# Feed-forward keys and receptance in two scaled float16 parts, and a fourth buffer for the attention probabilities

## The chip, the cores and the metric

The kernel runs on one core of one Trainium2 chip. The metric is device microseconds of one execution. The kernel before was run three times: 1599.81, 1601.11 and 1602.56 us, median 1601.11. One more execution was profiled: its own time is 1597.72 us, its span from the first to the last instruction 1595.9 us. The core has a matrix engine (TensorE, PE in the profile, with its weight loads shown as PEld), and VectorE (DVE), ScalarE (ACT), GpSimd (POOL) and a queue that issues transfers (SP).

## The reference

The input x has 4 rows of 2048 tokens with 256 channels. Four residual layers follow one another, each on a layer norm of x:

```python
x = x + attn_a(layernorm(x))      # (W n + b) of token 1 of each row, added to all its tokens
x = x + ffn(layernorm(x))         # weights W_r, W_k, W_v, mu_r, mu_k
x = x + attn_b(layernorm(x))      # 16 heads of 64, rotary positions, window of 128 back
x = x + ffn(layernorm(x))         # the same weights again
```

The feed-forward layer mixes each token n with the token before it:

```python
xr = mu_r * n + (1 - mu_r) * n_prev;   xk = mu_k * n + (1 - mu_k) * n_prev
out = sigmoid(xr @ W_r.T) * (relu(xk @ W_k.T) ** 2 @ W_v.T)
```

The attention attends in blocks of 128 tokens to the block itself and the one before, under a band mask, with a softmax.

## The kernel before, in words

The 8192 tokens are worked on in 32 groups of 256 (two tiles of 128). Each group passes through named stages, each of several steps: x (load, and the first layer's addition), f0 (first feed-forward), ln (layer norm for attention), v0 to v3 (values), q0 to q3 (queries and keys of four heads each, with rotary tables), s0 to s3 (attention of four heads each), o (output projection), f1 (second feed-forward), sv (store). The last group is split into two halves at its end (f1, f2 and w0, w1).

A matrix product in nearly float32 precision is made from parts: an operand a is cast to a hi part, and its lo part is a minus hi; three products hi x hi, hi x lo and lo x hi are summed in PSUM. In attention the parts are float16 and the weights are scaled by powers of two ahead of time. In the feed-forward layers of the kernel before all parts are float32r, four bytes each.

The steps of a feed-forward (class Ffn, lines 943 to 1123) are, with their engines: st sums of the norm (DVE), rs its scale (POOL), xn normalised tokens (ACT), tr transposes (PE), xt copy to SBUF and hs the column of the token before (ACT), d difference to the token before, xm and xo the mixes for receptance and key (DVE), xh hi part of both (ACT, 128x1024), xl lo part (POOL), pk keys (PE, 12 matmuls), pr receptance (PE, 12), rl relu, sq square, kh hi part of the keys (ACT), kl lo part (DVE), th tanh of half the receptance (ACT; the sigmoid is (1 + tanh)/2), pv values (PE, 12), sg the gate (DVE), ad addition to x (POOL).

The steps of an attention quarter (class Att, line 1332) are ks mask and sc scores into four PSUM banks (PE); for each head h of four m the maximum (DVE), e the exponential (ACT, two instructions in place in PSUM), h hi part (ACT) and l lo part (DVE) of the probabilities, into a tile phl for two heads; t0 and t1 the transposing transfers from phl to a tile pt (SP); av the product with the values (PE); i and n the division (DVE), ch and cl the parts of the context (ACT, POOL), tc its transposing transfer. In the queries and keys (class Qk, line 1223) qm and km are matmuls (PE), ka and kb the two products with the rotary tables (DVE), ad their sum (POOL), hi and lo the parts (ACT, POOL). For q1 the second product is made by ke (a copy on ACT) and mu (POOL). ks and kp hand keys on to the next group.

PSUM is divided into six single banks (tag pp) and one pair of banks (tag pair) which the query and key products and the context products take in turn. BUFS (line 38) gives the number of buffers of each tag; phl and pt have three each.

The order of the work is written out ahead by a planner (class Plan, line 143). Each step has a line in its class's SPEC with engine, duration in us, what it needs, which buffers it takes and which it gives back. The planner steps through a list schedule; among steps that could begin at about the same time on an engine the one with the lowest rank goes first. A rank is the group's number times PERIOD plus an entry of the table RANK (line 51), with another entry for each stage of the first and the last five groups. The instructions are then emitted in that order, each engine's queue keeps it, and waits are on the tiles that the instructions share. Since every instruction passes through one recording helper, nearly all have line 276 in the profile; tiles tell them apart: f_xm, f_xh, f_xl, f_pk, f_pr, f_kk, f_sg, f_pv belong to Ffn, at_s, at_mn, at_phl, at_pt, at_cx, at_c, at_ct to Att, qk_pd, qk_A, qk_B, qk_q, qk_k to Qk, pv to the values, po to the output. In the middle of the run several groups are in work at once: around group g's output stand s3 of group g+1, q0 of g+3 and f0 of g+4.

The class Setup (line 457) prepares the weights: the feed-forward steps there are fr, fk, fv (loads), mu (1 - mu), frh, fkh, fvh (hi parts, ACT), frl, fkl, fvl (lo parts, POOL), and fvs (W_v times 0.5, for the sigmoid).

Of the kernel before, what the change touches and what calls it, by code (L numbers as in the profile page):

```python
# [18 lines left out]
P = 128  # L19
C = 256  # L20
# [9 lines left out]
WSC = 256.0  # L30
EXPO = 0x7F800000
# [8 lines left out]
        "cs": 2, "A": 2, "B": 2, "q": 3, "k": 3, "mn": 3, "phl": 3, "pt": 3,  # L40
# [11 lines left out]
    "p.c1": -5056.91, "p.c2": 2969.02, "p.c3": -4885.05, "p.lv": -3111.05, "p.lb": -2925.83, "p.lw": -5009.81,  # L52
    "p.lo": -413.49, "p.lk": -2678.25, "p.lm": 2640.67, "p.lq": -3077.55, "p.fk": -1972.19, "p.fr": -2838.78,
    "p.fv": -777.00, "p.bd": -2779.47, "p.nvs": 3014.63, "p.nvm": 3072.90, "p.nvr": -2978.83, "p.nks": -788.22,
    "p.nkm": -4306.80, "p.nkr": -83.63, "p.nqs": -5037.35, "p.nqm": -4939.68, "p.nqr": -774.36, "p.sc": -472.11,
    "p.wv0": 570.16, "p.xv0": -201.89, "p.yv0": 3153.22, "p.zv0": -4686.76, "p.wv1": -2600.05, "p.xv1": -3342.91,
    "p.yv1": -610.29, "p.zv1": -4852.83, "p.wk0": -3021.86, "p.xk0": -1892.46, "p.yk0": -821.64, "p.zk0": -2369.83,
    "p.wk1": -2733.80, "p.xk1": -83.69, "p.yk1": -1953.56, "p.zk1": -2430.55, "p.wq0": -168.05, "p.xq0": 2297.47,
    "p.yq0": -4898.14, "p.zq0": -5081.41, "p.wq1": 2689.14, "p.xq1": -2913.52, "p.yq1": 3363.58, "p.zq1": -5071.63,
    "p.mk": -3071.43, "p.mu": -2906.24, "p.frh": -2530.67, "p.frl": -2423.55, "p.fkh": -2983.12, "p.fkl": 3185.31,  # L60
    "p.fvs": -769.81, "p.fvh": -4579.58, "p.fvl": 3091.15, "p.oq": -3006.79, "p.om": -204.90, "p.oc": -4648.57,
    "p.ox": -4580.42, "p.ob": -4965.08, "p.wo0": -613.03, "p.yo0": -2788.56, "p.zo0": -2882.62, "p.wo1": 3475.98,
    "p.yo1": -4703.07, "p.zo1": -4980.00, "r.ld": -5200.49, "r.st": 3455.58, "r.rs": -4687.73, "r.xn": 3456.91,
    "r.tr": 2907.19, "r.cp": -4814.90, "r.mm": 3513.18, "r.bi": -4976.56, "r.ad": -273.75, "x.ld": -4781.49,
    "x.a1": -513.94, "f0.st": -4882.63, "f0.rs": 2754.65, "f0.xn": 2986.21, "f0.tr": -4910.79, "f0.xt": -4990.79,
    "f0.hs": -3080.33, "f0.d": 2586.18, "f0.xm": -151.13, "f0.xo": -4611.65, "f0.xh": 976.57, "f0.xl": -4986.30,
    "f0.pk": -393.93, "f0.pr": -1868.76, "f0.rl": 3385.50, "f0.sq": 2308.38, "f0.kh": -5040.27, "f0.kl": -676.62,
    "f0.th": -6078.70, "f0.pv": 1034.70, "f0.sg": -4582.52, "f0.ad": 2796.64, "ln.st": -560.18, "ln.rs": -2135.71,
    "ln.xn": -358.88, "ln.hi": -845.47, "ln.lo": -4727.91, "ln.tr": -4597.42, "ln.cs": 1425.54, "tab.sc": 2955.10,
    "tab.st": -4548.65, "v0.mm": 1390.97, "v0.hi": -4851.14, "v0.lo": -952.76, "v1.mm": -2687.29,  # L70
    "v1.hi": -2644.64, "v1.lo": 2842.52, "v2.mm": 75.57, "v2.hi": -351.20, "v2.lo": -3081.42, "v3.mm": -4752.71,
    "v3.hi": -3057.25, "v3.lo": -4482.10, "q0.qm": -697.49, "q0.km": -1950.26, "q0.ka": -2699.89,
    "q0.kb": -5039.26, "q0.ad": 6.08, "q0.hi": -4974.92, "q0.lo": -5211.77, "q0.ks": -630.96, "q1.qm": -3584.31,
    "q1.km": -5189.02, "q1.ke": -5178.75, "q1.ka": -4943.18, "q1.mu": -992.72, "q1.ad": 1417.95, "q1.hi": 2888.04,
    "q1.lo": -4733.64, "q1.ks": -4326.00, "q2.qm": -468.39, "q2.km": -5058.89, "q2.ka": -2789.23,
    "q2.kb": -2972.37, "q2.ad": -2884.86, "q2.hi": 2658.83, "q2.lo": -924.24, "q2.ks": -2518.12, "q3.qm": 518.16,
    "q3.km": -4610.64, "q3.ka": 2530.62, "q3.kb": -4722.76, "q3.ad": -2764.39, "q3.hi": 2839.46, "q3.lo": -857.55,
    "q3.ks": -6086.78, "s0.k0": -1920.73, "s0.k1": -4586.15, "s0.k2": -613.21, "s0.k3": -2474.73,
    "s0.ks": -1923.23, "s0.sc": -3035.71, "s0.m0": -3099.45, "s0.m1": -3049.20, "s0.m2": -3015.22,
    "s0.m3": 2557.63, "s0.e0": -861.34, "s0.h0": -2876.34, "s0.l0": -2849.45, "s0.e1": 3370.73, "s0.h1": -2599.69,  # L80
    "s0.l1": 1349.23, "s0.t0": -2539.64, "s0.e2": 3083.70, "s0.h2": -1860.52, "s0.l2": 3055.36, "s0.e3": 2664.91,
    "s0.h3": -4879.42, "s0.l3": -610.50, "s0.t1": -4583.99, "s0.av": -4852.99, "s0.i0": 570.93, "s0.n0": -3079.20,
    "s0.ch": 2366.40, "s0.cl": -571.44, "s0.tc": -571.05, "s1.k0": -3309.12, "s1.k1": -1922.89, "s1.k2": -3002.20,
    "s1.k3": -2726.33, "s1.ks": -184.97, "s1.sc": -2823.37, "s1.m0": -2407.99, "s1.m1": -5176.15,
    "s1.m2": -1860.79, "s1.m3": 2664.46, "s1.e0": -2792.04, "s1.h0": -5036.68, "s1.l0": -5011.21,
    "s1.e1": -2759.97, "s1.h1": -2211.92, "s1.l1": -435.00, "s1.t0": -901.97, "s1.e2": 3228.18, "s1.h2": -2875.68,
    "s1.l2": -330.17, "s1.e3": -3095.98, "s1.h3": -4480.63, "s1.l3": -2400.51, "s1.t1": -40.32, "s1.av": -4976.07,
    "s1.i0": -302.67, "s1.n0": -5059.03, "s1.ch": -2945.71, "s1.cl": -4833.32, "s1.tc": -580.01, "s2.k0": -5104.06,
    "s2.k1": -2518.92, "s2.k2": -609.18, "s2.k3": -198.65, "s2.ks": -4270.64, "s2.sc": -3396.12, "s2.m0": -5359.90,
    "s2.m1": 3353.04, "s2.m2": -2954.66, "s2.m3": 2954.52, "s2.e0": -4801.17, "s2.h0": -4748.29, "s2.l0": -2533.65,  # L90
    "s2.e1": 2657.60, "s2.h1": -4876.22, "s2.l1": -143.77, "s2.t0": 3181.31, "s2.e2": -4740.23, "s2.h2": -1971.93,
    "s2.l2": -938.59, "s2.e3": 2929.40, "s2.h3": 3383.64, "s2.l3": -3250.26, "s2.t1": -4528.02, "s2.av": -3295.20,
    "s2.i0": -813.73, "s2.n0": -495.95, "s2.ch": -48.33, "s2.cl": 3091.26, "s2.tc": -696.74, "s3.k0": -677.40,
    "s3.k1": -3123.97, "s3.k2": -1933.84, "s3.k3": -465.00, "s3.ks": -4922.97, "s3.sc": -3446.85, "s3.m0": -798.61,
    "s3.m1": -4809.14, "s3.m2": 2876.12, "s3.m3": -4696.24, "s3.e0": -3417.38, "s3.h0": -4927.16,
    "s3.l0": -1999.52, "s3.e1": -4448.94, "s3.h1": -2880.18, "s3.l1": -280.82, "s3.t0": -2938.10,
    "s3.e2": -4878.66, "s3.h2": 3143.56, "s3.l2": -4964.39, "s3.e3": -4936.60, "s3.h3": -2514.89,
    "s3.l3": -1028.30, "s3.t1": -492.35, "s3.av": -2744.89, "s3.i0": 3016.46, "s3.n0": -1868.36, "s3.ch": 884.13,
# [195 lines left out]
def kernel(  # L294
# [69 lines left out]
    for nm in ("r", "k", "v"):  # L364
        FW[nm] = (
            cp.tile([P, 2, C], F32R, name=f"fw_{nm}_h"),
            cp.tile([P, 2, C], F32R, name=f"fw_{nm}_l"),
        )
# [1328 lines left out]
```

## Time and profile before

| what | value |
| --- | --- |
| median of three runs | 1601.11 us |
| profiled execution, own time | 1597.72 us |
| its span | 1595.9 us |
| PE busy | 1493.1 us, 94% |
| PE weight loads busy | 1241.3 us, 78% |
| DVE busy | 1438.1 us, 90% |
| ACT busy | 1345.6 us, 84% |
| POOL busy | 1317.3 us, 83% |
| mean granted TensorE clock | 0.991 |
| transfers | 248.23 MB, 156 GB/s |

A row of the profile's groups reads: line, engine, operation, tile written <- tiles read, shape and type, number of instructions | busy us in all, mean ns of one | idle us of the engine just before them, and what ended that idle time. Instructions of one engine overlap by some 0.05 to 0.1 us, so the sum of their lengths is more than the engine's busy time; the distance between two starts is the better price for one. Matmuls overlap far more: twelve f_pr of 280 ns take 1.43 us. The chain of work that ended last follows the waits back from the last instruction; a piece of it is a start, a length, and an engine with a tile.

### The profile page before, as it was taken

The page shows a single profiled execution, that of the slowest core. Times are in us where ns is not written, and L with a number is a line of the kernel's source. Part 1 is how long each engine was busy: PE and PEld are TensorE (multiplying, and loading weights), DVE is VectorE, ACT ScalarE, POOL GpSimd, SP SyncE. Part 2 cuts the span into 40 slices and gives each one's busy share as a digit, 9 for nine tenths or more (in the row PEclk, how much of TensorE's full clock was granted, in tenths as well). Part 3 has the DMA queues.
Part 4 walks back from the last instruction along what each step waited for, and adds up shares of the span by engine and source line. Part 5 has one row for each costly group of instructions (what it writes and reads, how often), then busy time and mean ns, then how long its engine had stood idle before and what let it go on. Part 6 is the DMA issues. An engine that isn't in the chain of part 4 may idle for free.

```text
span 1595.9 us, 55776 instructions
## 1 busy us (share of the span) xinstructions
PE 1493.1 (94%) x22887; PEld 1241.3 (78%) x22888; DVE 1438.1 (90%) x2607; ACT 1345.6 (84%) x2742; POOL 1317.3 (83%) x1409
## 2 busy tenths in 40 slices
PE   7989889999999999999999999999999999999976
PEld 4767778777777887887887878788887778887765
DVE  6889898999999999999999999999999999998973
ACT  5678788888988888898988889898888989888882
POOL 6899877788888888888888889888888988888732
PEclk9999999999999999999999999999999999999997
DMA  7059998889889799989798989997878989989781
GB/s 225 11 131 168 163 175 179 153 167 157 148 160 173 164 153 163 160 170 161 159 152 152 166 165 166 169 168 166 139 149 152 181 155 173 163 164 161 147 159 34
DMA packets 858831, 248.23 MB, mean 156 GB/s; under 512 B 822736, under 2 KB 857808, under 8 KB 858576
## 3 DMA queue, kind: packets, MB, share of 16 engines
q1 hardware_dynamic: 858144, 244.66, 82.3%
q8 instruction: 179, 2.93, 0.8%
q14 instruction: 76, 0.62, 0.1%
q10 hardware_dynamic: 432, 0.01, 0.0%
HBM read 42.22 MB, written 26.21 MB: 43 GB/s over the span
## 4 chain that ended last, share of the span: by engine, by line
PE 52%; DVE 18%; ACT 17%; POOL 7%; issue 6%; DMA 1%; DVEq 0%; ACTq 0%; SPq 0%; POOLq 0%
PE qk_pd L276 11%; PE po L276 9%; PE at_s L276 8%; PE pv L276 7%; PE at_cx L276 7%; PE f_pv L276 5%; ACT at_s L276 5%; DVE qk_A L276 3%; ACT at_phl L276 3%; DVE at_phl L276 3%; DVE at_mn L276 3%; PE f_pk L276 3%; PE f_pr L276 2%; DVE qk_B L276 2%; ACT f_xh L276 2%
## 5 line engine op out<-in xcount | busy, mean ns | idle before, releaser
L276 ACT ACTIVATE at_s<-at_s,at_mn 128x256 f32<-128x256 f32 x1024 | 462.7, 452 | 27.7 <-DVE at_mn L276 11.0
L276 DVE TENSOR_TENSOR at_phl<-at_s,at_phl 128x512 f16<-128x512 f32 x512 | 346.3, 682 | 40.3 <-ACT at_phl L276 37.1
L276 POOL TENSOR_TENSOR qk_A<-qk_A,qk_B 128x512 f32<-128x512 f32 x256 | 320.9, 1277 | 44.9 <-DVE qk_B L276 43.9
L276 DVE TENSOR_REDUCE at_mn<-at_s 128x2 f32<-128x512 f32 x512 | 325.3, 680 | 3.5 <-PE at_s L276 3.2
L276 ACT CAST at_phl<-at_s 128x512 f16<-128x512 f32 x512 | 300.6, 587 | 12.8 <-DMA at_pt<-at_phl 0.4
L276 PE MATMUL at_cx<-v,at_pt 128*128 128x65 f16 x5952 | 202.6, 194 | 37.3 <-DVE qk_B L276 24.5
L276 PEld LDWEIGHTS <-at_pt 128*128 128x128 f16 x5952 | 193.8, 98 | 52.0 <-issue 48.3
L276 POOL TENSOR_TENSOR at_ct<-at_c,at_ct 128x512 f16<-128x512 f32 x128 | 149.0, 1164 | 63.0 <-ACT at_ct L276 62.7
L276 PE MATMUL at_s<-qk_k,qk_q 32*128 32x256 f16 (+1 forms) x6144 | 189.7, 264 | 0.0
L276 PE MATMUL qk_pd<-a_xT,w_q_h 128*128 128x256 f16 x1024 | 176.3, 274 | 9.3 <-DVE at_c L276 3.8
L276 POOL TENSOR_TENSOR f_xl<-f_xm,f_xh 128x1024 fp32r<-128x1024 f32 x63 | 148.7, 2360 | 40.0 <-issue 24.9
L276 PE MATMUL po<-wo_h,at_ctT 128*128 128x256 f16 x1024 | 178.0, 273 | 1.0 <-DMA at_ctT<-at_ct 1.0
L276 DVE TENSOR_TENSOR qk_A<-qk_pd,a_cs 128x1024 f32<-128x1024 f32 x128 | 156.0, 1219 | 23.6 <-PE qk_pd L276 10.1
L276 PE MATMUL qk_pd<-a_xT,w_k_h 128*128 128x256 f16 x1024 | 176.8, 275 | 0.0
L276 PE MATMUL pv<-w_v_h,a_xT 128*128 128x512 f16 x512 | 161.7, 379 | 12.2 <-DVE at_phl L276 9.4
L276 PEld LDWEIGHTS <-at_ctT 128*128 128x128 f16 x1536 | 147.9, 98 | 18.1 <-DMA at_ctT<-at_ct 1.2
L276 PEld LDWEIGHTS <-qk_q 32*128 32x128 f16 x6144 | 153.4, 93 | 6.1
L276 POOL TENSOR_TENSOR qk_k<-qk_A,qk_k 128x512 f16<-128x512 f32 x128 | 149.4, 1167 | 0.0
L276 POOL TENSOR_TENSOR qk_q<-qk_A,qk_q 128x512 f16<-128x512 f32 x128 | 149.3, 1166 | 0.0
L276 PEld LDWEIGHTS <-a_xT 128*128 128x128 f16 x768 | 71.3, 98 | 98.9 <-DVE at_phl L276 16.9
L276 PE MATMUL qk_pd<-a_xT,w_k_l 128*128 128x256 f16 x512 | 140.6, 275 | 0.0
L276 PE MATMUL qk_pd<-a_xT,w_q_l 128*128 128x256 f16 x512 | 140.1, 274 | 0.0
(195 smaller groups left out, 3866.6 us busy)
## 6 DMA issues: line engine op xcount, KB each, us to landing
qk_kd<-qk_k SPq DMA_DIRECT2D x112, 128.0 KB, 2.4
qk_k<-qk_kd SPq DMA_DIRECT2D x112, 128.0 KB, 3.1
a_cs<-csd SPq DMA_DIRECT2D x24, 384.0 KB, 3.8
x<-in_x_dram SPq DMA_DIRECT2D x32, 256.0 KB, 3.6
out_dram<-x SPq DMA_DIRECT2D x31, 256.0 KB, 2.5
at_pt<-at_phl SPq DMA_TRANSPOSE x256, 4.5
a_cs<-in_cs_dram SPq DMA_DIRECT2D x32, 96.0 KB, 3.4
csd<-a_cs SPq DMA_DIRECT2D x8, 384.0 KB, 3.2
```

What stands on the lines that cost most here:

```text
L276: ins = fn(*a, **k)
```

## The change

1. The feed-forward weights W_r and W_k are kept as float16 parts, scaled: FSC = 8192 times a power of two taken from the norm of each matrix. The token mix (xh, xl) is kept in float16 parts as well, so pk and pr multiply float16 by float16. The weights W_v, the keys' parts kh and kl and the product pv stay float32r.
2. The normalised tokens are scaled through the norm: rs multiplies the variance by sig2, the square of a power of two taken from mu, in the instruction that adds epsilon. The scales are taken out again behind: th has a scale from a tensor, rsc, in place of 0.5, and fvs scales W_v by a tensor in place of 0.5.
3. Setup has four new steps: frn and fkn (squares of the two weights with a sum, ACT), fn (a matmul that sums over partitions, with one cast on DVE), fs (eleven small DVE instructions for the scales). mu has four more DVE instructions. frh, fkh and fvs need fs, and so does every rs of a feed-forward. frl and fkl move from POOL to DVE.
4. phl and pt have four buffers each in place of three.
5. The planner's durations follow (pk and pr 1.34 for 1.46, th .7 for .5, pv 1.5 for 1.46), and all 515 entries of RANK have other values, with four more for the new steps.

```diff
-        "cs": 2, "A": 2, "B": 2, "q": 3, "k": 3, "mn": 3, "phl": 3, "pt": 3,
+        "cs": 2, "A": 2, "B": 2, "q": 3, "k": 3, "mn": 3, "phl": 4, "pt": 4,
...
+        dt = F32R if nm == "v" else F16
+        FW[nm] = (cp.tile([P, 2, C], dt, name=f"fw_{nm}_h"), cp.tile([P, 2, C], dt, name=f"fw_{nm}_l"))
...
-        def scale(self, e):
+        def scale(self, e, over=None):
...
-            g.tensor_scalar(var, var, EPS, None, op0=ALU.add)
+            if over is None:
+                g.tensor_scalar(var, var, EPS, None, op0=ALU.add)
+            else:
+                g.tensor_scalar(var, var, EPS, over[:, 0:1], op0=ALU.add, op1=ALU.mult)
...
+        def norm_f(self, i, nm):
+            junk = FW[nm][0]
+            nc.scalar.activation(junk, W["f" + nm], AF.Square, accum_out=self.ffn[:, i : i + 1])
...
+        def fn(self):
+            f16 = small(2).bitcast(BF16)[:, :3]
+            nc.vector.tensor_copy(f16, self.ffn)
+            self.fsum = bank("pp", "fsum")[:, :3]
+            nc.tensor.matmul(self.fsum, ones, f16, start=True, stop=True)
...
+            else:
+                nc.scalar.mul(FW[nm][0], W["f" + nm], self.fw[:, i : i + 1])
...
+                nc.vector.scalar_tensor_tensor(l, w, self.fw[:, i : i + 1], h, op0=ALU.mult, op1=ALU.subtract)
...
-            nc.scalar.mul(W["fv"], W["fv"], 0.5)
+            nc.scalar.mul(W["fv"], W["fv"], self.fvsc[:, 0:1])
...
-        rs g 1.55 | st             |          |
+        rs g 1.55 | st p:fs        |          |
...
-        pk p 1.46 | xl p:fkl       | pp>pk kk>kk kh>kh kl>kl sg>sg |
-        pr p 1.46 | pk p:frl       | pp>pr    | xh xl
+        pk p 1.34 | xl p:fkl       | pp>pk kk>kk kh>kh kl>kl sg>sg |
+        pr p 1.34 | pk p:frl       | pp>pr    | xh xl
...
-            self.s.scale(nc.scalar)
+            self.s.scale(nc.scalar, sig2)
...
-            self.h = self.tokens("xh", 4, F32R)
+            self.h = self.tokens("xh", 4, F16)
...
-            self.l = self.tokens("xl", 4, F32R)
-            self.late("f.xl").tensor_tensor(self.l, self.m, self.h.bitcast(F32), op=ALU.subtract)
+            self.l = self.tokens("xl", 4, F16)
+            self.late("f.xl").tensor_tensor(self.l, self.m, self.h, op=ALU.subtract)
...
-            nc.scalar.activation(self.sig, self.r, AF.Tanh, scale=0.5)
+            nc.scalar.activation(self.sig, self.r, AF.Tanh, scale=rsc[:, 0:1])
```

The order in which the instructions stand in the queues, in the middle groups, is the same before and after but for neighbouring steps that change places. On DVE f1.st stands ahead of f0.xm, f1.sg behind s3.l1 and s3.l2, f1.d ahead of q0.ka, q1.ka ahead of s0.l3, and s1.l1 ahead of v1.lo; on ACT q0.hi ahead of f0.kh, s1.h1 ahead of v1.hi, q2.hi ahead of ln.hi; on PE q2.km inside the steps of s2; on POOL s0.cl ahead of ln.rs and q2.lo ahead of ln.lo; on SP q2.kp ahead of s1.tc. In the first and the last groups the orders differ more.

## The prediction

> **What bounds the kernel now.** The windows view first, for a stretch between two equal places of the schedule nine groups apart (the starts of two of q3's projections), then the page's busy shares and chain, then the chain in order of time, then the waits of TensorE, then the groups of instructions with shapes kept apart.
>
> ```profile
> 584.35:1002.80 418.45, 403.70 (x6385) 339.92 (x6386) 394.02 (x712) 369.29 (x756) 367.18 (x384) 1.00 0.89 161
> 1460.00:1574.70 114.70, 96.01 (x1587) 82.36 (x1579) 84.56 (x147) 83.75 (x171) 60.46 (x61) 0.96 0.79 139
> ```
>
> Columns: stretch and length, then busy us of PE, PEld, DVE, ACT, POOL, granted clock, DMA share, GB/s. The first row is nine groups: 418.45 / 9 = 46.5 us each, of which PE is busy 44.9, DVE 43.8, ACT 41.0, POOL 40.8. No engine has much room: PE idles 1.6 us of a group, DVE 2.7. The second row is the drain, where PE idles 18.7 us in all.
>
> ```profile
> PE 52%; DVE 18%; ACT 17%; POOL 7%; issue 6%; DMA 1%; DVEq 0%; ACTq 0%; SPq 0%; POOLq 0%
> PE qk_pd L276 11%; PE po L276 9%; PE at_s L276 8%; PE pv L276 7%; PE at_cx L276 7%; PE f_pv L276 5%; ACT at_s L276 5%; DVE qk_A L276 3%; ACT at_phl L276 3%; DVE at_phl L276 3%; DVE at_mn L276 3%; PE f_pk L276 3%; PE f_pr L276 2%; DVE qk_B L276 2%; ACT f_xh L276 2%
> ```
>
> Half of the chain that ended last is TensorE. f_pk has 3% of the span there (48 us of some 96 us of it), f_pr 2% (32 of 92): about half and a third of these two steps lie on the path.
>
> ```profile
> 716.91 2.73 PE po L276 x25
> 721.09 1.50 PE f_pk L276 x12
> 724.45 2.73 PE qk_pd L276 x24
> 727.17 1.42 PE f_pv L276 x12
> 728.59 1.43 PE f_pr L276 x12
> ...
> 743.66 1.14 DVE qk_A L276
> 744.82 0.59 ACT qk_B L276
> ...
> 750.42 2.76 PE pv L276 x12
> ```
>
> The chain (start, us, what) runs on TensorE from the values (pv) to the receptance (f_pr), about 27 us, then over ACT and mostly DVE for 20 us, and back to TensorE through the bank that the last at_phl frees. The float32r steps go at 0.119 us a matmul (1.43 / 12), float16 with the same 256 columns at 0.109 (2.73 / 25 in po).
>
> ```profile
> PE at_cx L276 <- DVE qk_B L276: 5.8, 8, 1.5
> PE pv L276 <- DVE at_phl L276: 3.0, 4, 0.8
> PE at_cx L276 <- DVE qk_A L276: 2.4, 4, 0.6
> PE at_cx L276 <- ACT qk_B L276: 2.1, 4, 0.8
> ```
>
> These are TensorE's waits in the same nine groups (total, times, longest). All are for PSUM: the one "pair" that projections and context share (10.3 us), and the banks "pp". None is for a transposed probability tile.
>
> ```profile
> L276 PE MATMUL po<-wo_h,at_ctT 128*128 128x256 f16 x1024 | 178.0, 273 | 1.0 <-DMA at_ctT<-at_ct 1.0
> L276 PE MATMUL f_pr<-fw_r_h,f_xl 128*128 128x256 f32 x256 | 71.7, 280 | 0.0
> L276 POOL TENSOR_TENSOR f_xl<-f_xm,f_xh 128x1024 fp32r<-128x1024 f32 x63 | 148.7, 2360 | 40.0 <-issue 24.9 <-ACT f_xh L276 11.7 <-POOL qk_A L276 1.8
> L276 POOL TENSOR_TENSOR qk_q<-qk_A,qk_q 128x512 f16<-128x512 f32 x128 | 149.3, 1166 | 0.0
> L276 POOL TENSOR_TENSOR qk_A<-qk_A,qk_B 128x512 f32<-128x512 f32 x256 | 320.9, 1277 | 44.9 <-DVE qk_B L276 43.9
> L276 ACT ACTIVATE wo_h<-u_o,small 128x256 f16<-128x256 f32 x8 | 3.1, 480 | 3.8 <-DVE small L276 3.8
> L276 ACT COPY f_xnT<-f_pt 128x256 f32<-128x256 f32 x2 | 0.7, 372 | 0.8 <-PE f_pt L276 0.8
> ```
>
> **The change part by part.** The sum is a difference against the profiled execution (span 1595.9, its own time 1597.72); the median of the runs shown, 1601.11, is 3.4 us (0.2%) above it, and I take the difference from the median.
>
> *Keys and receptance in float16.* Each feed-forward step has 24 such matmuls. pr: 1.43 to 12 x 0.109 = 1.31, so 0.12 less. pk: 1.50 to between 1.31 and 1.38 (its first matmul pays a change of weight form that po and qk_pd do not show), 0.17 less. TensorE loses 64 x 0.29 = 18.6 us. By the chain's shares, a half of pk's and a third of pr's lie on the path: 64 x (0.17 x 0.5 + 0.12 x 0.35) = 8.1 us. The rest is absorbed: behind f_pr of the second layer TensorE waited 0.60 us at 730.60 for DVE's qk_B to free the pair, and behind f_pr of the first layer qk_pd started at 739.90, just after that qk_B ended at 739.70. A shorter pr there only lengthens the wait. Bounds: 0 (all absorbed) to 18.6; taken 8.
>
> *Hi and lo parts of the mix.* xh on ACT keeps its elements: 128x512 casts from SBUF take 621 ns to f16 (at_ct) and 602 to 621 to fp32r (fw); 0. xl on POOL: the 4-byte rows 1277 (512 elements) and 2360 (1024) leave 194 ns fixed, so float16 at 1024 comes to 2 x 1166 - 194 = 2138, 0.22 less, 14 us of POOL in 63 of them. POOL carries 7% of the chain against 84% busy, one part in twelve: 1 us. Bounds 0 and 14.
>
> A rule speaks against this. The Trainium skill (GPSIMD Engine Reference, section 3.1, Elementwise) gives two-input tensor_tensor a floor of about 2.6 cycles an element set by the read port, not by the type; by it xl would save nothing. The rows 1166 against 1277 differ by type, and I go by them; by the rule the sum would be 1 us smaller.
>
> *Tanh with its scale in a tensor.* wo_h, a PSUM read with a scale per partition, takes 480 ns, the copy of 256 PSUM elements 372: 0.11 more, 65 x 0.11 = 7 us of ACT. In one of the two chain stretches I read (780 to 791 and 838 to 883 us) f_sg stands on ACT's part of the chain, in the other (730) it overlaps the next step. With ACT's 17% of the chain against 84% busy it is a fifth, 1.4; because the DVE step sg waits for it (19 waits, 3.9 us) I take 2. Bounds 0 and 7. The Trainium skill (ScalarE: Activation LUTs, What ACT_TABLE_LOAD costs) gives about 93 ns for each such operand; by it the 65 cost 6.0 us.
>
> *Variance scaled by sig2.* One operand becomes a pointer in a 220 ns POOL instruction, two columns wide. The 3x256 instruction with a pointer took 468 ns, the 3x256 cast 388: 0 to 0.08 each, at most 5 us of POOL; one part in twelve, 0.4, taken 0.
>
> *Order.* All ranks differ, yet in the middle groups the queues of before and after agree step for step, but for a few neighbours. The ones that count: on DVE q1.ka now stands ahead of s0.l3 (0.60 us between starts), f1.d ahead of q0.ka, and f1.sg behind two at_phl, so it no longer waits for tanh (0.21 us at 730.67); on ACT q0.hi is ahead of f0.kh; on PE q2.km stands inside s2's bank steps; on POOL and SP two neighbours each swap (ln.lo behind q2.lo, q2.kp ahead of s1.tc). q1.ka releases q1.ke on ACT, which leads by s1.e0 and s1.h0 to the at_phl that TensorE waited for at 750.42. That stretch was on the chain in three of the five groups from 727 to 960 us. f1.d ahead of q0.ka delays q0.kb, which frees the pair for q1.qm, by 0.6: TensorE then starts q1 later by some 0.5, but q1.ka (743.6 before) had 1.0 us to spare behind q1's matmuls. So 0.60 x 0.5 of 28 steady groups is 8 us, less 1 for the swaps that push a step back; 7 taken. Bounds: the same 0.6 lost in all groups through q0.kb (+17) and won in all (-17).
>
> *Four tiles each.* ACT waited for a probability tile once (0.4 us in the page's group of casts), TensorE never for a transposed one. 0; the cover is the three tiles there already. Nothing more than 0.4 can be won, and space for it comes from the halved xh, xl and weights.
>
> *Setup.* Two squares with sums on ACT (0.63 + 0.19 each, as the rows of ld_v and junk), one matmul, 16 small DVE steps at 0.12 to 0.2 us (3 us), then every f0.rs waits for fs. Keys and receptance weights are now loaded 2nd and 7th on SP, before most attention weights. Before, the first f0.rs ran at 17.8 us; fs needs the loads (about 9), the squares and the matmul behind nvm, so about 15. DVE has fewer weight steps ahead of the first f0.d (29.7 us), and the lo parts of the two weights move from POOL (1.27 each) to DVE (0.7 each). Between -3 and +4; taken 0.
>
> *Ends.* Fill and drain orders do differ. PE idles 49 us in 0 to 161 and 1460 to 1596; moving an eighth of that either way is 6 us. Taken 0, kept for the range.
>
> Sum: -8 - 1 + 2 - 7 = -14. 1601.1 - 14 = 1587.
>
> **The rivals.**
> 1. *Absorbed.* DVE, which loses nothing, sets the pace through the pair. For: 10.3 us of TensorE's waits are for it, and DVE ran without a gap from 731 to 744 us. Against: PE has 52% of the chain. Then only order (7) against tanh and swaps (7) remains: 1601, within 3 us.
> 2. *Slower: ACT.* From 838 to 883 us the chain is ACT alone, almost without idle. If ACT closes the cycle, both tanh of a group (0.22) lie on it, 7 us, and if q0.kb's 0.6 shift takes the q1.ka gain back there is nothing against it: 1608. It decides once order gains less than 0.2 us a group and the pair absorbs TensorE's gain. Against: ACT idles 5.5 us of 46.5 in the same groups.
> 3. *All of it counts.* TensorE's 0.58 a group and the 0.6 of q1.ka in every steady group: 46.5 to 45.3, 28 x 1.2 = 33 us: 1568. Against: DVE would have to run at 43.8 of 45.3.
> 4. *float16 matmuls no faster here,* because f_pv between them stays float32r and each change costs. Bound: gain of pk and pr halves, 1591; inside the forecast.
>
> **How the numbers follow.** Forecast (with 4) 0.66, absorbed 0.13, slower 0.13, all 0.08. The forecast's own range is 1575 to 1598: the chain's gain between 3 and 15, order 0 to 12. With the ends' 6 us and half of rivals 1 and 2, the range is 1572 to 1603. About 0.2% is what a measurement can tell from no change: under 1597.9 is faster (forecast less a little, and all: 0.76), to 1604.3 the same (0.10), above it slower (0.14).
>
> **What would show it.** In the profile after: f_pk and f_pr at 273 ns with separate weight loads of 98 ns; f_xl near 2140 and f_sg near 700 ns; nine middle groups in 412 to 415 us; TensorE's waits for the pair grown, not shrunk. Wrong if the middle groups keep 418 us with PE idle up by 4 (absorbed), if ACT's idle falls while the group grows (rival 2), or if the middle gains but the first po moves from 161 us or the drain from 136 us by more than 6.

## The result, and the profile after

The changed kernel takes 1608.0 us (median of ten runs, 1603.29 to 1613.91) against 1602.19 us for the kernel before, measured beside it: ratio 1.0037, 95% interval 1.0023 to 1.0051. It is slower by about 6 us; 1587 was predicted and the range ended at 1603. The profiled execution took 1606.72 us, its span is 1604.9, 9.0 more than that of before.

First the table that carries the comparison. It is read from the ends of the output projections (`po`) in the profiled executions, one of each kernel here and below, in us: the first output, the fifth, the nineteen middle groups from the fifth to the 24th output, the last eight groups, and what follows.

| kernel | first | fifth | 19 middle groups | last 8 | rest | span |
| --- | --- | --- | --- | --- | --- | --- |
| before | 166.6 | 347.0 | 883.7 | 344.3 | 20.9 | 1595.9 |
| after | 160.8 | 351.7 | 884.9 | 348.0 | 20.4 | 1604.9 |
| difference | -5.8 | +4.7 | +1.2 | +3.7 | -0.5 | +9.0 |

The middle, where the gain was to come from, gained nothing; the ends lost 7.9 us in these two profiles. In the nineteen middle groups the granted clock was 1.00 in both, so they can be compared to the microsecond: two kernels with the same steps and order there (after and old_fill, further down) took 884.9 and 885.0 us, two others (f16_old_order and f16_old_cs3) 883.4 and 883.9. The last eight groups can't be, since the granted clock falls there, and not equally in each profile. after_cs3 and old_fill (see The ends) have the changed kernel's order there and took 342.1 and 342.7 us. The 5.9 us between after and after_cs3 lie in three groups, 47.9, 37.5 and 27.4 us in place of 46.5, 35.5 and 24.9, at a granted clock of 0.96, 0.95 and 0.81 in place of 1.00, 1.00 and 0.93. So the +3.7 is not shown to be the order's.

The windows view of the profile after, for nine groups between two outputs and for the drain. Columns as before: stretch, length, busy us of PE, PEld, DVE, ACT, POOL, granted clock, DMA share, GB/s.

```profile
398.10:817.70 419.60, 399.91 (x6388) 326.81 (x6385) 396.51 (x709) 371.27 (x755) 362.83 (x382) 1.00 0.91 159
1470.00:1584.70 114.70, 99.29 (x1552) 81.24 (x1540) 84.78 (x150) 83.58 (x170) 63.37 (x64) 0.94 0.80 140
```

TensorE is busy 399.9 us of nine groups in place of 403.7, yet the groups take 419.6 in place of 418.5. It idles 19.7 us where it idled 14.8: the time taken from it went into waiting.

The groups of instructions in the profile after, shapes kept apart, that answer to those shown of before:

```profile
L277 PE MATMUL po<-wo_h,at_ctT 128*128 128x256 f16 x1024 | 179.3, 274 | 0.4 <-DMA at_ctT<-at_ct 0.4
L277 PE MATMUL f_pr<-fw_r_h,f_xl 128*128 128x256 f16 x256 | 70.6, 276 | 0.0
L277 POOL TENSOR_TENSOR f_xl<-f_xm,f_xh 128x1024 f16<-128x1024 f32 x63 | 134.4, 2133 | 38.0 <-issue 20.6 <-ACT f_xh L277 10.8 <-POOL qk_A L277 5.4
L277 ACT ACTIVATE f_sg<-f_pr,rsc 128x512 f32<-128x512 f32 x63 | 43.3, 687 | 3.0 <-PE f_pr L277 2.7
L277 POOL TENSOR_SCALAR f_mv<-f_mv,sig 128x2 f32<-128x2 f32 x63 | 16.8, 266 | 19.0 <-DVE f_mv L277 15.2 <-DVE at_ri L277 0.4
```

The durations came out close to those worked out: f_pr 276 ns like po, f_xl 2133 (2138 forecast), the tanh f_sg 687 (700 forecast, 593 before), the variance 266 (220 before). What failed is what these durations are worth.

The chain's shares on the page of after, by engine and then by line:

```profile
PE 47%; DVE 27%; ACT 15%; issue 5%; DMA 2%; POOL 2%; SPq 1%; ACTq 0%; DVEq 0%; POOLq 0%
```

TensorE fell from 52% to 47%, DVE rose from 18% to 27%. The same chain in order of time (start, us, what), in one of the middle groups:

```profile
648.92 1.13 DVE qk_A L277
650.05 0.59 DVE qk_B L277
...
652.38 1.56 DVE f_xm L277 x4
...
654.60 1.91 PE at_s L277 x58
656.50 0.84 PE at_cx L277 x24
657.36 0.60 ACT qk_q L277
657.97 0.52 ACT qk_k L277
658.49 0.49 ACT f_kh L277
659.00 0.70 DVE f_kl L277
659.74 4.21 PE pv L277 x18
...
679.12 1.31 PE f_pk L277 x12
680.42 1.86 PE at_s L277 x68
```

Twelve keys take 1.31 us (1.50 before), as forecast. New is the way into pv: the hi part of queries and keys (qk_q, qk_k) now stands ahead of f_kh on ACT, and pv waits for f_kl behind it. TensorE's waits in the nine groups of 398.1 to 817.7 us (total, times, longest) show the same:

```profile
PE at_cx L277 <- DVE qk_B L277: 8.5, 8, 1.9
PE qk_pd L277 <- DVE qk_B L277: 4.8, 9, 1.3
PE pv L277 <- DVE f_kl L277: 4.7, 9, 0.8
```

The second is the shift of q0.kb by f1.d on DVE, which the prediction had at "some 0.5" a group and called covered: 4.8 / 9 = 0.53. The third was 0.3 in all in nine groups of before, from 394 to 812.9 us:

```profile
PE pv L276 <- DVE f_kl L276: 0.3, 1, 0.3
```

### The profile page after: what moved, and what is told of

Its sections match the earlier page's. It is cut to its first block, busy times and chain, and to the rows that moved or that the text cites. A ratio compares the mean times of both kernels' runs of the same rounds, so it can differ in the third digit from the quotient of the medians.

```text
span 1604.9 us, 55756 instructions
## 1 busy us (share of the span) xinstructions
PE 1487.3 (93%) x22889; PEld 1200.3 (75%) x22889; DVE 1449.4 (90%) x2625; ACT 1353.7 (84%) x2746; POOL 1303.6 (81%) x1407
## 4 chain that ended last, share of the span: by engine, by line
PE 47%; DVE 27%; ACT 15%; issue 5%; DMA 2%; POOL 2%; SPq 1%; ACTq 0%; DVEq 0%; POOLq 0%
PE qk_pd L277 10%; PE po L277 9%; PE pv L277 7%; PE at_s L277 7%; DVE at_mn L277 6%; PE at_cx L277 6%; DVE qk_A L277 6%; DVE qk_B L277 4%; ACT at_s L277 4%; DVE at_phl L277 4%; PE f_pv L277 3%; ACT at_phl L277 3%; DVE f_xm L277 2%; ACT qk_q L277 1%; ACT qk_k L277 1%
## 5 line engine op out<-in xcount | busy, mean ns | idle before, releaser
L277 PE MATMUL pv<-w_v_h,a_xT 128*128 128x512 f16 x512 | 168.0, 379 | 14.0 <-DVE f_kl L277 11.6
L277 POOL TENSOR_TENSOR f_xl<-f_xm,f_xh 128x1024 f16<-128x1024 f32 x63 | 134.4, 2133 | 38.0 <-issue 20.6
L277 PE MATMUL po<-wo_l,at_ctT 128*128 128x256 f16 x512 | 140.0, 273 | 0.0
```

What stands on the lines that cost most here:

```text
L277: ins = fn(*a, **k)
```

## The experiments

### The order and the arithmetic taken apart

f16_old_order keeps the changed arithmetic, the buffers and the new setup steps, and emits the steps in the order of the kernel before; f32_new_order is the reverse, float32r with the changed order and four buffers for pt, as this order needs, with one for bn (the norm's sums) to make room.

```diff
-        return [b[2] for b in self.begun]
+        return [ops[key][2] for key in ORDER]   # the other kernel's order, written out
```

> The float16 arithmetic of the changed kernel with its queues in the order of the kernel before (the two weight loads and the new setup steps put ahead of the first norm). Theory A, the new order costs and float16 gains: 1590 to 1597 us, nine middle groups in 412 to 416 us. Theory B, float16 is absorbed behind DVE and the pair of PSUM banks, and the order costs 6 us: 1600 to 1604, nine middle groups in 418 to 420. Theory C, the float16 arithmetic itself costs (setup, tanh with a tensor scale): 1606 or more.

> The float32r arithmetic of the kernel before with its queues in the order of the changed kernel (four tiles for the transposed probabilities as that order needs, three for the others, one buffer for the norm's sums to make room). Theory A: 1612 to 1622 us, slower than both. Theory B: 1606 to 1610, as the changed kernel. Theory C: 1600 to 1604, as the kernel before.

Measured: f16_old_order 1602.51 us, ratio to the kernel before 1.0007 (0.9998 to 1.0015); f32_new_order 1615.34, ratio 1.0083 (1.0070 to 1.0097).

| kernel | first | fifth | 19 middle groups | last 8 | rest |
| --- | --- | --- | --- | --- | --- |
| f16_old_order | 170.0 | 354.5 | 883.4 | 344.7 | 19.1 |
| f32_new_order | 166.2 | 357.6 | 888.3 | 344.8 | 22.9 |

The first came out as its theory B has it, the second as its theory A. Whether the one buffer for bn adds to the second was not tried. In the old order float16 leaves the middle where it was (883.4 against 883.7). The new order costs 13 us with float32r and about 5 with float16. With float32r 10.6 us of it stand ahead of the fifth output (357.6 against 347.0) and 4.6 in the nineteen middle groups. So the order, forecast at -7, is the loss, and the float16 kernel gains a part of that back only in the order that loses: by the two ratios 7 us from f32_new_order to after. Of that, in the profiles, 5.4 us stand ahead of the first output (166.2 to 160.8) and 3.4 in the middle (888.3 to 884.9). The windows view of f16_old_order over nine groups, and TensorE's largest wait there:

```profile
400.00:818.70 418.70, 400.35 (x6386) 329.02 (x6385) 394.17 (x711) 371.03 (x755) 362.66 (x381) 1.00 0.92 160
```

```profile
PE at_cx L492 <- DVE qk_B L492: 7.9, 8, 1.9
```

That wait was 5.8 us before: TensorE comes to the pair earlier and waits there.

### Two neighbours put back

new_kh puts f0.kh ahead of q0.hi on ACT again in the middle groups; new_kh_d also puts f1.d behind q0.kb on DVE.

```diff
+MOVES = [("f0.kh", ("q0.hi", -1), False), ("f1.d", ("q0.kb", 3), True)]   # new_kh: the first alone
+        for key, other, behind in MOVES:
+            for g in range(4, 27):
+                ...
+                    order.remove(a)
+                    order.insert(order.index(b) + behind, a)
```

> The changed kernel with one step moved in groups 4 to 26: on ACT the hi part of the keys (f0.kh) ahead of the cast of q0's queries and keys (q0.hi), as before. The chain after runs over q0.hi, f0.kh and f0.kl to TensorE's pv; TensorE waited 4.7 us for f_kl in nine groups. If that swap costs: 0.3 to 0.5 us a group less, 1597 to 1601 us. If the chain goes another way at once: 1605 to 1610.

> As new_kh, and on DVE the difference f1.d behind q0.kb as before, in groups 4 to 26; TensorE's waits of 4.8 us in nine groups for qk_B ahead of q1's projections should go. If both swaps cost: 0.6 to 1.0 us a group less, 1586 to 1594 us. If DVE sets the pace either way: 1603 to 1610.

Measured: new_kh 1610.29 us, ratio 1.0060 (1.0047 to 1.0073), middle 887.2; new_kh_d 1604.93, ratio 1.0025 (1.0012 to 1.0039), middle 884.6. TensorE's waits in nine groups, of new_kh (399.6 to 820.4 us) and then of new_kh_d (399.6 to 819.1):

```profile
PE pv L286 <- DVE at_phl L286: 7.0, 9, 1.0
PE qk_pd L286 <- DVE qk_B L286: 4.8, 9, 1.3
```

```profile
PE pv L286 <- DVE at_phl L286: 6.3, 9, 0.9
PE qk_pd L286 <- DVE qk_B L286: 1.2, 2, 0.7
```

Moving f0.kh alone removes no time: pv then waits 7.0 us for at_phl where it waited 4.7 for f_kl, and the middle grows by 2.3 us (the ratios, 1.0060 and 1.0037, have intervals that just overlap). f1.d does cost: from new_kh to new_kh_d the wait for qk_B falls from 4.8 to 1.2 us, the middle by 2.6 us and the whole by 0.35%, 5 us. At one granted clock, 0.986 to 0.987, the difference is 3 to 5. f1.d was not moved by itself, so what it costs in the changed kernel as it stands is not shown. The prediction had exactly this step and let it go as covered by "1.0 us to spare". Both edits together come to 0.12% below the changed kernel, with intervals that overlap: the forecast for the case that both swaps cost, 1586 to 1594, was missed by 11 us.

### What a microsecond is worth on each engine

These kernels shorten one engine's work in the groups, with the order unchanged: f_d left out (DVE, 0.67 us twice a group), the square of the keys left out (ACT, 0.63 twice), tanh with a constant scale (ACT, 0.09 twice), three of 25 matmuls of each half of po left out (TensorE, 0.65 a group). The ones named f16 have the changed arithmetic in the order of before.

```diff
-            nc.vector.tensor_tensor(self.dx, self.T[:, :, : self.nt], self.pt, op=ALU.subtract)
+            self.dx = self.T[:, :, : self.nt]                     # f32_no_d, f16_no_d, and both _d_sq
...
-            nc.scalar.activation(self.k, self.kk, AF.Square)
+            pass                                                  # f32_no_sq, and both _d_sq
...
-            nc.scalar.activation(self.sig, self.r, AF.Tanh, scale=rsc[:, 0:1])
+            nc.scalar.activation(self.sig, self.r, AF.Tanh, scale=0.5)            # f16_tanh_const
...
-for l, w in ((0, wh), (0, wl), (1, wh))):
+for l, w in ((0, wh), (0, wl), (1, wh))[: 3 - (kt > 4)]):         # f32_po22
```

> The kernel before (float32r, its own order), with one DVE step left out of every feed-forward: f_d, the difference to the token before (0.67 us, twice a group, 1.34 us of DVE's 43.8 a group); the mix is then made from the shifted tokens themselves, so this part of the computation is left out. It goes with f16_no_d. Theory B (in the middle a path through DVE and ACT is within 0.3 us of a group as long as the path through TensorE, so a cut of one alone shows little): the nine groups behind the sixth output, 418.8 us before, come to 416 to 418.8; whole 1590 to 1601. Theory R1 (DVE alone sets the pace, TensorE's time does not count): 407 to 411 us, whole 1565 to 1575. Theory R2 (ACT sets the pace, neither DVE nor TensorE counts): 418.8, whole 1601.

> The same step f_d left out of the changed kernel's arithmetic in the order of the kernel before (the run f16_old_order, 418.7 us for nine groups). Theory B: with the cover of DVE shortened, the 0.58 us of a group that the float16 steps save on TensorE show, by a third to all of them: 2 to 5 us less in nine groups than f32_no_d, and 6 to 18 us less in the whole. Theory R1: the same nine groups as f32_no_d within 0.5 us. Theory R2: 418.8 for both.

> f16_old_order with the constant 0.5 as tanh's scale in place of the tensor (the scale of the keys' and receptance weights is then not taken out of the receptance: this part is left out). ACT loses 0.09 us twice a group. Theory B: the tanh is no part of what sets the pace: nine groups 418.2 to 418.9, whole within 2 us of f16_old_order. Theory T (the float16 gain is there and the slower tanh eats it up): nine groups 414 to 417, whole 6 to 12 us less.

> The kernel before, float32r and its own order, with three of the 25 matmuls left out of each half of the output projection (the lo part of the weights for three of eight row blocks): 6 x 0.109 = 0.65 us of TensorE a group, about what float16 keys and receptance save in a group (0.58). In the chains of before, f16_old_order and f16_no_d each group has one stretch of some 20 us in which TensorE runs alone, back to back (pv, qk_pd, at_s, f_pv, at_cx, po, f_pt, po, at_cx), without f_pk and f_pr, and one of 26 us in which TensorE, DVE and ACT have paths of nearly equal length. Theory B (time counts only where TensorE runs alone): the whole cut counts here, nine groups 412.5 to 414 us in place of 418.8, whole 1576 to 1584. Theory R2 (TensorE does not count, ACT sets the pace): 418 to 418.8, whole 1598 to 1601.

> f16_no_d with the square of the keys left out as well (ACT, 0.63 us twice a group), so that all three parallel paths of the long stretch are shorter: TensorE by 0.58, DVE by 1.34, ACT by 1.26 us a group. Theory B: at most what TensorE saves, at least half of it: nine groups 412.5 to 415.5 us (f16_no_d 417.7), whole 1577 to 1588. Theory P (something else, as the transposing transfers, holds the group at 46.4 us): 417 us or more, whole 1594 or more.

> The kernel before (float32r) with both f_d and the square of the keys left out, the twin of f16_no_d_sq (nine groups 413.9 us, nineteen 872.9). Theory B (float16's TensorE time counts once the DVE and the ACT path are both shorter): nineteen groups 876 to 881 us, nine 415.5 to 417.5, whole 1587 to 1592, the difference to the twin being a third to all of 19 x 0.58 us. Theory A1 (ACT alone held the group, TensorE's time is worth nothing even now): nineteen 872.5 to 874, nine 413.5 to 414.3, whole 1579 to 1583.

> The kernel before with only the square of the keys left out (ACT 1.26 us a group). Theory B (with ACT shorter, DVE's and TensorE's paths still hold the group): nine groups 417 to 418.6 us, whole 1595 to 1600. Theory A1 (ACT closes the cycle by itself): 413.5 to 415, whole 1582 to 1588.

| kernel | cut from 19 groups | 19 middle groups | gain of it | ratio to before |
| --- | --- | --- | --- | --- |
| before | | 883.7 | | |
| f16_old_order | PE 11.0 at f_pk, f_pr | 883.4 | 0.3 | 1.0007 (0.9998 to 1.0015) |
| f16_tanh_const | the same, ACT 0.19 a group less | 882.2 | 1.5 | 0.9996 (0.9987 to 1.0004) |
| f32_po22 | PE 12.4 at po | 877.3 | 6.4 | 0.9933 (0.9922 to 0.9945) |
| f32_no_d | DVE 25.5 | 881.9 | 1.8 | 0.9956 (0.9944 to 0.9968) |
| f16_no_d | DVE 25.5, PE 11.0 | 881.1 | 2.6 | 0.9976 (0.9968 to 0.9985) |
| f32_no_sq | ACT 23.9 | 876.1 | 7.6 | 0.9910 (0.9897 to 0.9924) |
| f32_no_d_sq | ACT 23.9, DVE 25.5 | 874.8 | 8.9 | 0.9886 (0.9873 to 0.9900) |
| f16_no_d_sq | ACT 23.9, DVE 25.5, PE 11.0 | 872.9 | 10.8 | 0.9893 (0.9879 to 0.9908) |

The cut is the cut of one group times 19. The ratios hold the fill as well, where float16 in the old order is late (fifth output 349.6 us in f16_no_d_sq, 341.5 in f32_no_d_sq; more of that below), so the worth in the groups is read from the middle. A difference of half a microsecond there means nothing, by the pairs above. Read down, this prices the engines in the middle of this kernel:

- TensorE time in the output projection is worth half of itself or more (6.4 of 12.4). One of f32_po22's groups, from 485.8 to 534.3 us, ran at a granted clock of 0.96 and took 48.5 us; in before it took 46.9 at 1.00. With about 2 us for that, an estimate, the worth is two thirds. The same engine's time in keys and receptance is worth little in the order of before: 0.3 of 11.0 with the slower tanh in it, 1.5 with the constant scale (f16_tanh_const), and, with the slower tanh, 0.8 with f_d gone (881.9 to 881.1) and 1.9 with the squares gone too (874.8 to 872.9). In the changed order all the float16 edits together are worth 3.4 (888.3 to 884.9).
- ACT's time is worth a third of itself, at the squares (7.6 of 23.9) and, less surely, at the tanh (1.2 of 3.6, 883.4 to 882.2). The square also stands between the keys and pv, so its 7.6 us hold ACT's time and the length of that path, which no run takes apart.
- DVE's is worth a fourteenth (1.8 of 25.5), though DVE is busy 94% of these groups. POOL's was not measured.

The chain of f16_old_order shows why the place counts. One stretch of a middle group, and the next:

```profile
663.07 4.04 PE pv L492 x18
667.11 2.62 PE qk_pd L492 x24
669.73 1.86 PE at_s L492 x68
671.59 1.62 PE f_pv L492 x12
673.22 1.46 PE at_cx L492 x48
674.68 2.73 PE po L492 x25
...
677.84 2.73 PE po L492 x25
680.57 1.47 PE at_cx L492 x48
682.30 0.70 DVE at_c L492
683.03 0.62 ACT at_ct L492
684.18 0.61 ACT f_pk L492
684.81 0.59 ACT f_kh L492
686.04 2.47 DVE at_mn L492 x4
```

From 663 to 682 us TensorE works without a gap and the chain has no other way; po stands there, f_pk and f_pr do not. Behind it the chain of before went on over TensorE with f_pk and f_pr; here it goes over DVE and ACT (in this group, further on, also over 4.7 us of a table's transfer), and the group is no shorter. TensorE's f_pk and f_pr are nowhere on this chain in the nineteen groups; on that of before they hold 45 us. So by the chain of before these two steps were on the path, and beside them lay another of nearly the same length.

My theory for these runs, that time counts only where TensorE runs alone and that three parallel paths are equal elsewhere, stands only in part. f32_no_sq went against it (415.4 us in nine groups, 417 to 418.6 forecast, 413.5 to 415 if ACT alone closed the cycle), and with all covers shorter float16 was worth 1.9 of 11.0 and not a third. By these prices ACT is nearest to being alone beside TensorE's stretch, and DVE and the keys' TensorE time lie under it. f16_no_d against f32_no_d came out as theory R1 has it, TensorE's time not counting (0.2 us in nine groups, 2 to 5 forecast). And even at po a third to a half of the cut was lost (416.5 us in nine groups, with the one of 48.5 at the lower clock, where 412.5 to 414 was forecast): f32_po22's chain goes 11 us over POOL in the group shown.

```profile
659.82 1.16 POOL at_ct L276
660.98 2.45 POOL qk_A L276 x2
...
666.32 1.26 POOL qk_A L276
667.58 1.11 POOL qk_q L276
668.69 1.12 POOL qk_k L276
669.81 1.24 POOL x L276
```

### The ends

after_cs3 gives the changed kernel a third buffer for the rotary tables. old_fill takes the order of f16_old_order up to the fifth output and the changed order from there; old_drain takes the changed order up to the output of group 22 and the old one from there. f16_old_cs3 is f16_old_order with the third table buffer and the table loads of groups 3 to 7 issued earlier.

```diff
-        "cs": 2, "A": 2, "B": 2, "q": 3, "k": 3, "mn": 3, "phl": 4, "pt": 4,
+        "cs": 3, "A": 2, "B": 2, "q": 3, "k": 3, "mn": 3, "phl": 3, "pt": 4,
```

> The changed kernel with its own order written out, a third buffer for the rotary tables (cs 3 in place of 2) and three for the probabilities (phl 3 in place of 4, which the order never uses more of). In the profile after, the table of a group in the first row is loaded when q3's second product of two groups before is done, and ACT waits 6.4 us for it. Theory F (this turn lengthens the first groups): that wait falls under 2 us, the fifth output comes at 346 to 349 us in place of 351.7, whole 1602 to 1605. Theory O (the order of the first groups costs by other waits): fifth output at 350 or later, whole 1606 to 1609.

> The changed kernel's arithmetic, with the order of f16_old_order up to the output of the fifth group and the changed kernel's order from there. Theory S (the order's loss is spread: middle groups at the ends of the rows and the last groups, with no gain in the first groups): 1605 to 1609, as the changed kernel or 2 us below. Theory F (the loss is in the first groups): 1601 to 1603.

> The changed kernel with its own order up to the output of group 22 and the order of f16_old_order from there. Theory S: the last groups lose their 3 to 4 us against f16_old_order: 1603 to 1605. Theory F: 1606 to 1609, as the changed kernel.

> f16_old_order with a third buffer for the rotary tables (phl 3 in place of 4) and the loads of the tables of groups 3 to 7 put some 90 to 140 steps earlier, behind the first key transfer of two groups before. In f16_old_order the table of group 5 was issued 4.6 us behind the step that frees its buffer, TensorE's context product ran at a granted clock of 0.66 just behind, and that group took 52.5 us in place of 46.6. Theory F (the table's wait makes that): 46.5 to 48 us there, fifth output at 347 to 350, whole 4 to 6 us less than f16_old_order, ratio to the kernel before 0.997 to 0.9985. Theory O (another wait holds it): 51 us or more, ratio 1.000 to 1.002.

| kernel | us | ratio to before | first | fifth | 19 middle groups | last 8 |
| --- | --- | --- | --- | --- | --- | --- |
| after_cs3 | 1606.65 | 1.0040 (1.0026 to 1.0054) | 161.7 | 352.7 | 886.0 | 342.1 |
| old_fill | 1603.60 | 1.0020 (1.0011 to 1.0030) | 169.5 | 353.5 | 885.0 | 342.7 |
| old_drain | 1604.10 | 1.0021 (1.0012 to 1.0030) | 162.0 | 352.1 | 885.5 | 344.0 |
| f16_old_cs3 | 1598.33 | 0.9982 (0.9973 to 0.9991) | 171.3 | 349.0 | 883.9 | 344.9 |

The third buffer does nothing for the changed kernel: ACT still waited 3.8 us for tables in the first 260 us (4.1 in after), with the loads at the same place in SP's queue, and the fifth output came at 352.7. With the loads moved as well, in the old order, the group that took 52.5 us in f16_old_order takes 45.6, and the fifth output comes at 349.0. Which of the two edits did it was not separated. TensorE's granted clock in that group was 0.87 in f16_old_order (0.53 from 224.0 to 238.5 us) and 1.00 in f16_old_cs3, so the 7 us hold the lower clock as well as the waits. Among the waits of f16_old_order from 205 to 235 us are these:

```profile
POOL at_ct L492 <- ACT at_ct L492: 7.1, 3, 4.4
DVE qk_A L492 <- POOL qk_k L492: 3.4, 1, 3.4
ACT at_ct L492 <- DVE at_c L492: 3.0, 1, 3.0
PE at_cx L492 <- DVE qk_B L492: 2.6, 1, 2.6
ACT a_cs L492 <- DMA a_cs<-in_cs_dram: 2.6, 1, 2.6
```

f16_old_cs3 is the one kernel here that leaves nothing out and is faster than both before and after: by 0.18% against before.

By their ratios old_fill and old_drain are each about 0.16%, 2.6 us, below the changed kernel, with intervals that overlap its own (1.0023 to 1.0051). Neither settles where the ends lose: old_fill's fifth output comes no earlier (353.5), and old_drain's last eight groups, 344.0 us, are no shorter than the 342.1 and 342.7 that the changed order takes in after_cs3 and old_fill. In the profiles the loss ahead of the fifth output stands in the second group, 57.0 to 58.3 us in after, after_cs3 and old_drain against 49.6 before. In the middle the loss has a place too: the changed kernel's groups take 46.3 us on average, 0.2 less than before, but the two at a change of row (from one of the four rows of x to the next, every eight groups) 48.0 and 47.3, where before had 46.7 and 46.4; that is some 2 us at each of the two changes of row among the nineteen. Which swap makes it was not tried.

### Work moved off ACT

Since ACT's time was worth a third, the last two runs moved the square to POOL, with the computation whole.

```diff
-            nc.scalar.activation(self.k, self.kk, AF.Square)
+            nc.gpsimd.tensor_tensor(self.kk, self.kk, self.kk, op=ALU.mult)   # sq_pool_f1: f1 alone
+            self.k = self.kk
```

> f16_old_cs3 with the square of the keys moved from ACT (0.63 us from PSUM to PSUM) to POOL (in place in SBUF, at most the 1.28 us of its other 128x512 float32 steps), both times in a group; kh and kl then read SBUF. ACT loses 1.26 us of 41, POOL gains 2.5 on 40.4 of 46.4. Theory A (ACT's time counts, POOL has room): nineteen middle groups 876 to 879 us in place of 883.9, whole 1588 to 1593. Theory Q (POOL's queue or the 0.65 us longer way to kl take it back): 882 to 890, whole 1597 to 1606.

> The same for the second feed-forward alone. Theory A: half of it, 880 to 881.5 us, whole 1592 to 1596. Theory Q: 883 to 887, whole 1597 to 1602.

sq_pool took 1686.82 us, ratio 1.0533 (1.0519 to 1.0548), middle 935.7; sq_pool_f1 1635.51, ratio 1.0211 (1.0197 to 1.0225), middle 907.1. Both are far above even the losing forecast. From the waits of sq_pool in 420 us of the middle, 500 to 920, and then two of its groups of instructions:

```profile
ACT f_kh L492 <- POOL f_kk L492: 30.5, 17, 2.8
PE at_cx L492 <- DVE qk_B L492: 17.2, 8, 2.6
DVE f_kl L492 <- ACT f_kh L492: 15.5, 16, 1.2
```

```profile
L492 POOL TENSOR_TENSOR f_kk<-f_kk 128x512 f32<-128x512 f32 x63 | 65.6, 1041 | 5.9 <-ACT f_kk L492 5.7
L492 DVE TENSOR_TENSOR f_kl<-f_kk,f_kh 128x512 fp32r<-128x512 f32 x63 | 60.0, 953 | 58.4 <-ACT f_kh L492 58.4
```

ACT was relieved of 0.63 us and then stood 30.5 / 17 = 1.8 us in its queue at each f_kh, because the order has f_kh where ACT's own square used to end. The price list above holds for work that disappears, not for work that comes back with a wait.

## Why the prediction was wrong, point by point

**Keys and receptance, -8.** This step failed. The durations were right to the hundredth (1.31 us for twelve), the weight was not: "by the chain's shares, a half of pk's and a third of pr's lie on the path". In the order of before the runs give 0.3 to 1.9 us of 11.0 in nineteen groups, so 3 to 17% and not 43%; over all groups 0.5 to 3 us. With the slower tanh taken out it is 1.5, 14%. In the changed order all the float16 edits together gave 3.4 in those groups, 31%. Nothing is seen of the change of weight form for which the prediction left pk room up to 1.38. A share of one chain says where the chain went, not how much shorter the group gets when the step shrinks. The prediction's own sign of rival 1, the middle groups staying at 418 us with TensorE's idle time up by 4, is what was seen: 419.6 us, idle up by 4.9.

**Order, -7.** This step failed too, in sign: +13 us with float32r, about +5 with float16. It priced one swap (q1.ka ahead of s0.l3) by what it released and called another (f1.d ahead of q0.ka) covered. All that the groups away from a change of row gained is 0.2 us (46.3 against 46.5), with float16 in it. The second delays TensorE by the 0.53 us that was named, and it was not covered: with f0.kh put back, putting it back as well was worth 2.6 us in the nineteen groups and 5 in all. Of the changes of row, some 4 us in the nineteen groups, nothing was said.

**Ends, 0 with 6 either way.** The two profiles give +7.9, outside the 6; with after_cs3's profile in place of after's it is +3.3. The first output came 5.8 us earlier and the second group took that back and more (58.3 us in place of 49.6), the fifth was 4.7 late. The last groups' +3.7 came at a lower clock; the same order took 2 us less than before in after_cs3 and old_fill.

**Tanh, +2.** Right: 0.09 us a step, 1.2 us in nineteen groups, 1.8 us in the whole by the two ratios (1.0007 and 0.9996, with intervals that overlap). The Trainium skill (ScalarE: Activation LUTs, What ACT_TABLE_LOAD costs) gives about 93 ns for a scale that is read through a pointer; 593 to 687 ns is 94.

**Parts of the mix, -1.** The duration was right (2133 ns, 2138 forecast); its worth was not measured by itself. The prediction took one twelfth from POOL's 7% of the chain and 84% busy; the profile's page has 83%, which changes nothing. The Trainium skill (GPSIMD Engine Reference, section 3.1, Elementwise) gives about 2.6 cycles an element for a two-input tensor_tensor, as a floor of the read port. It names no dependence on the type, which the prediction read as none; the same 128x1024 step went from 2360 to 2133 ns, so for this step the type counts.

**Four tiles, 0, variance, 0, setup, 0.** Four tiles: right for the probabilities, since after_cs3 with three of them (and a third table buffer) agrees with the changed kernel (1.0040 and 1.0037); the four transposed ones were not tried apart. The variance step took 46 ns more, inside its bounds; its worth was not measured. Setup was not measured by itself: the first output is 5.8 us earlier in the new order and 3.4 later in f16_old_order, where the new steps were put in by hand.

**The rivals.** Rival 1, absorbed, describes the middle and gave 1601; f16_old_order, which is that case without the new order, took 1602.5. Rival 2 gave 1608, the measured time. Its ground was in part misread: from 838 to 883 us the chain of before is not ACT alone, but runs over POOL from 846.20 to 857.42 and over DVE to 861.7. Half of its mechanism has support, ACT has the highest worth of the engines beside TensorE that were tried, but its price was made of 7 us for the tanh, which cost 1.8; the rest came from the order. Its number was met by other terms, which is luck.

## What to carry to other kernels

Before pricing a step by its share of the chain, look at what the chain does beside it: where one engine runs without a gap for 20 us and every chain passes there, a microsecond was worth half or more here; where three engines are busy together it was worth between a thirtieth and a third, at 94% busy or not. Leaving a step out, on each engine in turn, measures this in a few runs, and it should be done before the arithmetic is changed. A regenerated order is an edit of its own and should be measured apart from the arithmetic that comes with it: here it cost more than the arithmetic could give.

## What the runs showed of the hardware

The time of one and the same kernel goes with the mean clock that TensorE was granted; which of the two leads was not tried. Of 23 runs of the kernel before beside f32_no_d, the four at 0.990 to 0.991 took 1597.1 to 1599.4 us, the five at 0.985 1600.8 to 1602.2; the changed kernel went from 1603.3 at 0.990 to 1613.9 at 0.983. The profiled execution of before had 0.991 and that of after 0.987, so, by the runs of before at 0.987 (1600.1 on average) and the three fastest at 0.990 to 0.991 (1597.2), some 3 of the 9.0 us between their spans go with the clock, an estimate. In the nineteen middle groups the granted clock was 1.00 in every kernel but the two with the square on POOL, apart from one short drop each in f32_po22 and after_cs3; the lower clock stands in the first and the last groups. It also limits two readings above: eight of old_fill's twelve runs had 0.989 or more and took 1601.0 to 1604.3, the other four 1606.4 to 1608.8, as the changed kernel at that clock; and at 0.988 to 0.989 f16_old_cs3 (1598.7 to 1599.9) is within 1 us of the kernel before (1598.9 to 1600.2), so that most of its 0.18% lies in having had the higher clock more often. Whether the order of the first groups brings the higher clock or chance did was not settled.

A square in place on POOL took 1041 ns for 128x512 float32, the same engine's sum of two tiles of that size 1273. The DVE step f_kl took 953 ns with both operands in SBUF while POOL was at work, 687 with one of them in PSUM (f16_old_cs3); f_xl, of the same size on DVE from two SBUF operands, took 691 in the last groups. What lengthens it was not tried.
